# Products of field pairs by blocks in place of one row after another, and one PSUM tile of eight banks in place of eight buffers

## The chip, the cores and the metric

The kernel runs on one core of a Trainium2 chip. The metric is the device time of one execution in microseconds (us); the profile's span is about 1.9 us shorter. All runs told here were fast (no execution over 1.5% above the fastest of its kernel). A claim of "faster" or "slower" is made at 2%, with a 95% interval.

Names in the profile: PE is TensorE (matmuls), PEld its weight loads, DVE is VectorE, ACTq and SPq are the queues from which ScalarE and SyncE issue transfers. In the list of DMA queues, q1 carries the stores and the first two tiles' loads, q10 the other loads. The granted clock is TensorE's clock as a share of full speed. The ramp is the start of the program, until the first two tiles are under way; a fill is VectorE's work on one output buffer.

## The reference

```python
vid = jnp.einsum('bfd,de->bfe', x, W)          # x: (4096, 32, 64), W: (64, 64)
idx_i, idx_j = jnp.triu_indices(32, k=1)       # 496 pairs i < j
return x[:, idx_i, :] * vid[:, idx_j, :]       # (4096, 496, 64) float32
```

The output is 520 MB, the input 34 MB. There is one multiplication for each output element.

## The kernel before

The batch is cut into 16 tiles of 2 x 128 rows. In a tile, partitions are 2 halves x 64 embedding elements, and the free dimensions are fields (F = 32) and 128 batch rows (C). An output buffer (SLOT) holds 124 of the 496 pairs, so a tile fills four, and there are three of them. PSUM is the memory that matmuls write; four fields of `vid` fill one of its eight banks.

```python
    xpool = ctx.enter_context(tc.tile_pool(name="x", bufs=2))
    opool = ctx.enter_context(tc.tile_pool(name="out", bufs=3))
    psum = ctx.enter_context(
        tc.tile_pool(name="ps", bufs=8, space=bass.MemoryType.PSUM)
    )
    ...                                    # load(): x of a tile, in 4 pieces of 8 fields
    for t in range(NT):
        if 0 < t < NT - 1:
            loaded.append(load(t + 1, 4, nc.scalar))
        xt = loaded[t]
        vid = []
        for b in range(0, F, BANK):        # BANK = 4 fields, one PSUM bank
            pv = psum.tile([P, BANK, C], F32, tag="pv", name=f"pv_{t}_{b}")
            ...                            # two matmuls, one for each half of the partitions
            vid.append(pv)
        sent = 0
        for j in range(1, F):
            i = 0
            while i < j:
                ...                        # n pairs (i .. i+n-1, j), until the row or the buffer ends
                nc.vector.tensor_tensor(
                    ot[:, at - base : at - base + n, :],
                    xt[:, i : i + n, :],
                    vid[j // BANK][:, j % BANK : j % BANK + 1, :].to_broadcast([P, n, C]),
                    ALU.mult,
                )
                i += n
                at += n
                if t * NP + at == until or at in (base + SLOT, NP):
                    nc.sync.dma_start(     # the store: a whole buffer, in the first two tiles less
                        out=out[t][:, sent:at, :],
                        in_=ot[:, sent - base : at - base, :],
                    )
                    ...
```

## Time and profile before

| | before |
|---|---|
| time, median (lowest to highest) of 3 runs | 1298.64 us (1297.97 to 1299.37) |
| span of the profiled run | 1296.3 us |
| VectorE: instructions, busy | 544, 1098.1 us (85%) |
| VectorE: idle before its instructions | 158.3 us |
| TensorE: matmuls, busy | 512, 225.5 us |
| moved | 553.81 MB |

### The profile page before, as it was taken

What the parts mean: (1) busy time and instruction counts of PE and PEld (TensorE: products, weight loads), DVE (VectorE), ACT (ScalarE), POOL (GpSimd) and SP (SyncE); (2) the same over time, 40 slices, a digit from 0 to 9 for tenths busy, and PEclk for the clock granted to TensorE, in tenths of its full rate; (3) what the DMA queues carried; (4) which work ended last, traced back from release to release, by engine and by line L of the source; (5) the groups of instructions that cost most, each with busy time, mean ns of one, the idle gap of its engine ahead of it and who ended that gap; (6) DMA issues with size and microseconds to landing.
All of it is one profiled execution on the core that took longest, in us unless ns stands there. A gap on an engine that the chain in (4) does not pass through costs nothing.

```text
span 1296.3 us, 2062 instructions
## 1 busy us (share of the span) xinstructions
PE 225.5 (17%) x512; PEld 52.1 (4%) x512; DVE 1098.1 (85%) x544; POOL 0.2 (0%) x4
## 2 busy tenths in 40 slices
PE   4112131122121121211212112121121211212000
PEld 1000000000000000000000000000000000000000
DVE  7999999898798888988888888888888888979970
POOL 0000000000000000000000000000000000000000
PEclk8555555565555555655555565555555655555555
DMA  9999999999999999999999999999999999999996
GB/s 379 430 426 433 438 432 425 434 434 434 428 432 432 434 432 434 431 434 436 432 434 434 426 434 432 430 432 432 432 433 431 434 432 434 432 431 443 425 431 288
DMA packets 20891, 553.81 MB, mean 427 GB/s; under 512 B 2448, under 2 KB 2448, under 8 KB 10256
## 3 DMA queue, kind: packets, MB, share of 16 engines
q1 hardware_dynamic: 12816, 524.33, 93.8%
q10 hardware_dynamic: 8064, 29.36, 5.5%
q8 instruction: 4, 0.07, 0.0%
q14 instruction: 7, 0.06, 0.0%
HBM read 33.59 MB, written 520.09 MB: 427 GB/s over the span
## 4 chain that ended last, share of the span: by engine, by line
DMA 61%; DVE 34%; issue 1%; DVEq 0%; PE 0%; SPq 0%
DMA out_dram<-o 61%; DVE o L99 34%; DMA x<-in_r_x_dram 0%; DVEq L145 0%; PE pv L81 0%; DVEq L99 0%; SPq L56 0%
## 5 line engine op out<-in xcount | busy, mean ns | idle before, releaser
L99 DVE TENSOR_TENSOR o<-x,pv 128x2176 f32<-128x2176 f32 (+27 forms) x544 | 1098.1, 2093 | 158.3 <-DMA out_dram<-o 149.5
L81 PE MATMUL pv<-x,w 64*64 64x512 f32 x512 | 225.5, 1025 | 966.3 <-DMA x<-in_r_x_dram 887.2
L81 PEld LDWEIGHTS pv<-x,w 64*64 64x64 f32 x512 | 52.1, 208 | 1138.0 <-issue 1137.4
L128 POOL MEMSET const-bfloat16-1.0<- 128x1 bf16 x1 | 0.1, 102 | 0.0
L128 POOL MEMSET const-uint8-127<- 128x1 uint8 x1 | 0.1, 102 | 0.0
L128 POOL MEMSET const-float32-1.0<- 128x1 f32 x1 | 0.1, 99 | 0.0
L128 POOL MEMSET const-float32-0.0<- 128x1 f32 x1 | 0.1, 98 | 0.2 <-issue 0.2
## 6 DMA issues: line engine op xcount, KB each, us to landing
out_dram<-o SPq DMA_DIRECT2D x56, 7936.0 KB, 42.9
x<-in_r_x_dram ACTq DMA_DIRECT2D x56, 512.0 KB, 48.7
out_dram<-o SPq DMA_DIRECT2D x2, 3008.0 KB, 17.8
out_dram<-o SPq DMA_DIRECT2D x1, 5952.0 KB, 27.1
out_dram<-o SPq DMA_DIRECT2D x1, 4928.0 KB, 23.1
out_dram<-o SPq DMA_DIRECT2D x1, 4416.0 KB, 19.0
out_dram<-o SPq DMA_DIRECT2D x1, 4224.0 KB, 21.2
out_dram<-o SPq DMA_DIRECT2D x1, 3904.0 KB, 15.3
```

The lines of the kernel that those rows point to most:

```text
L81: nc.tensor.matmul(pv[half, :, :], lhsT=w2[half, :], rhs=xt[half, b : b + BANK, :], start=True, stop=True,)
L99: nc.vector.tensor_tensor(ot[:, at - base : at - base + n, :], xt[:, i : i + n, :], vid[j // BANK][:, j % BANK : j % BANK + 1, :].to_broad ...
L128: nc = _bacc.Bacc("TRN2", target_bir_lowering=False, num_devices=1, dynamic_dma_scratch_size=1024)
```

## The change

The intent is fewer VectorE instructions. In the old order each field j gives a row of j products, and buffer ends cut some, so 34 instructions a tile. In the new order pairs are grouped so that one instruction covers a block: within 16 fields, the pairs inside groups of 2, then across halves of groups of 4, of 8, of 16, and between the two 16s one block of 16 x 16. That is 22 instructions a tile. A block needs `vid` of fields in several banks at once, so `vid` becomes one tile over all eight banks. The first two tiles, whose stores start small and grow, keep the old order. The core of the diff:

```diff
+def by_block():
+    def within(lo):
+        yield "step", lo, 2, 1, 0
+        for k in range(2):
+            yield "step", lo, 4, 2, k
+        for k in range(4):
+            yield "step", lo, 8, 4, k
+        yield "row", lo + 8, lo, 8, 8
+    yield from within(0)
+    yield "row", 16, 0, 16, 16
+    yield from within(16)
 ...
-        tc.tile_pool(name="ps", bufs=8, space=bass.MemoryType.PSUM)
+        tc.tile_pool(name="ps", bufs=1, space=bass.MemoryType.PSUM)
     )
+    vid = psum.tile([P, F, C], F32)
 ...
-            pv = psum.tile([P, BANK, C], F32, tag="pv", name=f"pv_{t}_{b}")
 ...
-                    pv[half, :, :],
+                    vid[half, b : b + BANK, :],
 ...
-        for j in range(1, F):
-            ...
+        for at, m, w, i, di, j, dj in products(by_field() if t < 2 else by_block()):
+            ...
+            if m == 1:
+                left = xt[:, i : i + w, :]
+                right = vid[:, j : j + 1, :].to_broadcast([P, w, C])
+            else:
+                o = o.rearrange("p (m w) c -> p m w c", m=m)
+                right = vid[:, j : j + (m - 1) * dj + 1 : dj, :].unsqueeze(2).to_broadcast([P, m, w, C])
+                if di == 0:
+                    left = xt[:, i : i + w, :].unsqueeze(1).to_broadcast([P, m, w, C])
+                else:
+                    left = xt.rearrange("p (m d) c -> p m d c", d=di)[:, i // di : i // di + m, i % di : i % di + w, :]
+            nc.vector.tensor_tensor(o, left, right, ALU.mult)
```

`products` (cut here) cuts blocks where a buffer ends. The host undoes the new order of the pairs.

More of the change, by code (lines that the diff above doesn't have):

```diff
@@ L20, with by_field, products, pairs @@
 ]
-def first(j):
-    return j * (j - 1) // 2
+def by_field():
+    return [("row", j, 0, 1, j) for j in range(1, 32)]
+def by_block():
[9 more added lines that the diff above has]
+    yield from within(16)
+def products(blocks):
+    at = 0
+    for kind, a, b, c, d in blocks:
+        if kind == "row":
+            rows, n, i0, di, j0, dj = c, d, b, 0, a, 1
+        else:
+            rows, n, i0, di, j0, dj = 16 // b, c, a, b, a + c + d, b
+        r = k = 0
+        while r < rows:
+            room = SLOT - at % SLOT
+            if k or room < n:
+                m, w = 1, min(n - k, room)
+            else:
+                m, w = min(rows - r, room // n), n
+            yield at, m, w, i0 + r * di + k, di, j0 + r * dj, dj
+            at += m * w
+            if w == n or k + w == n:
+                r, k = r + m, 0
+            else:
+                k += w
+def pairs(blocks):
+    for at, m, w, i, di, j, dj in products(blocks):
+        for r in range(m):
+            for k in range(w):
+                yield i + r * di + k, j + r * dj
 @with_exitstack
@@ L73, in pairwise_bilinear_kernel @@
         xt = loaded[t]
-        vid = []
         for b in range(0, F, BANK):
-            pv = psum.tile([P, BANK, C], F32, tag="pv", name=f"pv_{t}_{b}")
             for h in range(2):
@@ L87, in pairwise_bilinear_kernel @@
                 )
-            vid.append(pv)
         sent = 0
-        for j in range(1, F):
-            i = 0
-            while i < j:
-                at = first(j) + i
-                base = at - at % SLOT
-                if at == base:
-                    ot = opool.tile([P, SLOT, C], F32, tag="o", name=f"o_{t}_{at}")
-                n = min(j - i, base + SLOT - at)
-                nc.vector.tensor_tensor(
-                    ot[:, at - base : at - base + n, :],
-                    xt[:, i : i + n, :],
-                    vid[j // BANK][:, j % BANK : j % BANK + 1, :].to_broadcast([P, n, C]),
-                    ALU.mult,
-                )
-                i += n
-                at += n
-                if t * NP + at == until or at in (base + SLOT, NP):
-                    nc.sync.dma_start(
-                        out=out[t][:, sent:at, :],
-                        in_=ot[:, sent - base : at - base, :],
-                    )
-                    sent = at
-                    if t * NP + at == until:
-                        until += next(growing, NT * NP)
+        for at, m, w, i, di, j, dj in products(by_field() if t < 2 else by_block()):
+            base = at - at % SLOT
+            if at == base:
+                ot = opool.tile([P, SLOT, C], F32, tag="o", name=f"o_{t}_{at}")
+            n = m * w
+            o = ot[:, at - base : at - base + n, :]
+            if m == 1:
+                left = xt[:, i : i + w, :]
+                right = vid[:, j : j + 1, :].to_broadcast([P, w, C])
+            else:
+                o = o.rearrange("p (m w) c -> p m w c", m=m)
+                right = vid[:, j : j + (m - 1) * dj + 1 : dj, :].unsqueeze(2).to_broadcast([P, m, w, C])
+                if di == 0:
+                    left = xt[:, i : i + w, :].unsqueeze(1).to_broadcast([P, m, w, C])
+                else:
+                    left = xt.rearrange("p (m d) c -> p m d c", d=di)[:, i // di : i // di + m, i % di : i % di + w, :]
+            nc.vector.tensor_tensor(o, left, right, ALU.mult)
+            at += n
+            if t * NP + at == until or at in (base + SLOT, NP):
+                nc.sync.dma_start(
+                    out=out[t][:, sent:at, :],
+                    in_=ot[:, sent - base : at - base, :],
+                )
+                sent = at
+                if t * NP + at == until:
+                    until += next(growing, NT * NP)
@@ L149 @@
     got = r.results[0]["out_0_dram"].reshape(NT, 2, D, _OUTS[0][0][1], C)
-    order = [first(j) + i for i in range(F) for j in range(i + 1, F)]
-    got = got.transpose(1, 0, 4, 3, 2)[:, :, :, order]
-    return _np.ascontiguousarray(got).reshape(_OUTS[0][0])
+    place = {p: k for k, p in enumerate((i, j) for i in range(F) for j in range(i + 1, F))}
+    res = _np.empty((2, NT, C, _OUTS[0][0][1], D), _np.float32)
+    for t in range(NT):
+        order = [place[p] for p in pairs(by_field() if t < 2 else by_block())]
+        res[:, t][:, :, order] = got[t].transpose(0, 3, 2, 1)
+    return res.reshape(_OUTS[0][0])
```

## The prediction

> **What bounds the kernel now.** I began with the page of the profile: the engines' busy time, the slices for the DMA engines, and the queues.
>
> ```profile
> PE 225.5 (17%) x512; PEld 52.1 (4%) x512; DVE 1098.1 (85%) x544; POOL 0.2 (0%) x4
> ...
> DMA  9999999999999999999999999999999999999996
> GB/s 379 430 426 433 438 432 425 434 434 434 428 432 432 434 432 434 431 434 436 432 434 434 426 434 432 430 432 432 432 433 431 434 432 434 432 431 443 425 431 288
> ...
> q1 hardware_dynamic: 12816, 524.33, 93.8%
> q10 hardware_dynamic: 8064, 29.36, 5.5%
> ```
>
> VectorE, which the change works on, is busy 85% of the span. The 16 DMA engines are busy at 90% or more in 39 of 40 slices, and the two data queues together take 93.8% + 5.5% = 99.3% of them. The rate is flat near 432 GB/s; only the first slice and the last differ much. So the DMA engines have about 0.7% of 1296.3 us, some 9 us, left, most of it at the two ends.
>
> The second view is the chain of waits in order of time, because its summary (DMA 61%, DVE 34%) could be read as if a third of the time were VectorE's to save.
>
> ```profile
> 698.38 17.67 DVE o L99 x16
> 716.06 42.61 DMA out_dram<-o
> 758.68 0.03 issue
> 758.73 0.04 issue
> 758.77 16.96 DVE o L99 x5
> 775.74 43.52 DMA out_dram<-o
> ...
> 819.36 17.02 DVE o L99 x6
> 836.40 44.37 DMA out_dram<-o
> ...
> 880.86 17.09 DVE o L99 x7
> ```
>
> The pattern is: VectorE fills one output buffer of 124 rows in about 17 us, the store of it lands some 43 us later, and its landing frees the buffer for a new fill. The chain visits every third buffer because there are three. A store of 7936 KB alone needs about 20 us of the DMA engines, so 43 us is two stores long: it queued behind an earlier one. The 17 us of VectorE in the chain lie beside other buffers' stores. If the fill ended sooner, the store would queue longer and land at the same time.
>
> Third, the waits between engines and the timeline of a steady tile:
>
> ```profile
> DVE o L99 <- DMA out_dram<-o: 149.5, 52, 5.0
> ```
>
> ```profile
> 536.80 17.66 DVE L99 TENSOR_TENSOR o<-x,pv 128x128 f32<-128x128 f32 x16 [3.16 <-DMA out_dram<-o]
> ...
> 541.74 3.68 PE L81 MATMUL pv<-x,w 64*64 64x512 f32 x8 [16.44 <-DMA x<-in_r_x_dram]
> ...
> 556.82 17.07 DVE L99 TENSOR_TENSOR o<-x,pv 128x1536 f32<-128x1536 f32 x7 [2.37 <-DMA out_dram<-o]
> ...
> 561.93 3.68 PE L81 MATMUL pv<-x,w 64*64 64x512 f32 x8 [16.51 <-DMA x<-in_r_x_dram]
> ...
> 582.03 3.68 PE L81 MATMUL pv<-x,w 64*64 64x512 f32 x8 [16.42 <-DMA x<-in_r_x_dram]
> ```
>
> At each buffer VectorE idles 2 to 3 us until an old store has landed; 149.5 of its 158.3 us of idle time are of this kind. The steady period of a tile follows from the chain: the fill of sixteen instructions starts at 698.38 and, three tiles later, at 940.82, so 242.44 / 3 = 80.8 us. VectorE needs 17.67 + 16.96 + 17.02 + 17.09 = 68.7 us of these. It could become 17% slower before it set the pace.
>
> **What the Trainium skill says.** "DMA: Bandwidth & Descriptors", section "Where 436 GB/s comes from", gives 435.2 GB/s as the ceiling of a core's 16 ports. The trace agrees: a window of three steady tiles moved 433 GB/s. The same section says that the HBM share of about 358 GB/s binds for transfers to and from HBM; this trace, of one core alone, does not show that. "VectorE: DVE Perf Modes", section "The TRN2 errata — SBUF-src ops pay a fixed extra latency per instruction", gives (N+151)/0.96 ns for an fp32 tensor_tensor, and its section "The perf-mode tier table (the rule you actually need)" one element a cycle for it whatever the memory. The groups by form agree:
>
> ```profile
> L99 DVE TENSOR_TENSOR o<-x,pv 128x3968 f32<-128x3968 f32 x16 | 68.5, 4281 | 0.0
> ...
> L99 DVE TENSOR_TENSOR o<-x,pv 128x128 f32<-128x128 f32 x16 | 4.6, 287 | 50.0 <-DMA out_dram<-o 41.7 <-PE pv L81 8.3
> ```
>
> The rule gives 4291 and 291 ns. "PSUM — Partial Sum Buffer", section "PSUM bank collisions raise a hardware error ⚠️", asks for synchronisation by bank, not by address. That decides what one tile of eight banks does; see below.
>
> **The change, part by part.** *Instructions.* From the third tile on there are 22 instead of 34 products a tile. The buffers of a tile get 9, 2, 2 and 9 of them instead of 16, 7, 6 and 5 in some order. All fills are 124 x 128 = 15872 elements, so the chain gives the exposed cost of one more instruction: (17.67 - 16.96) / (16 - 5) = 0.065 us, less than half of the fixed part in an instruction's own duration, because neighbours overlap. Twelve instructions fewer save 12 x 0.065 = 0.78 us a tile, 14 tiles 11 us. Busy VectorE goes from 1098 to about 1087 us, and the fills take about 17.2, 16.8, 16.8, 17.2 us. Those 11 us lie beside a store that ends later, so they come back as waiting: VectorE's idle time for stores goes from 149.5 to about 160 us. On the path to the end: 0.
>
> *Transfers.* Rows leave in another order, but in the same buffers of 124 rows and the same 7936 KB per store; loads keep their four pieces. 553.81 MB stays. The first two tiles, with their growing stores, keep their old order. So the ramp stays as well: 0.
>
> *PSUM.* One tile of eight banks takes the place of eight one-bank buffers. In the built list of instructions the matmuls of the changed kernel still wait bank by bank, or piece by piece, for VectorE, and products wait for matmuls in steps too. What moves is when a bank comes free. Banks 0 to 3 are free after row 120 of 496. Banks 4 and 5 are read until the last block of the tile, and banks 6 and 7 to its end. The loads' pieces arrive 20 us apart; counting 32 matmuls a tile, the group at 541.74 is the fourth piece of the tile whose products begin at 536.80. So the pieces come 55, 35 and 15 us before the start, and 5 us after it. The changed order needs the first two pieces at the start (35 us in hand less 4 us of matmuls), the third at row 120, 17 us in, and the fourth at row 248, two buffers or 40 us in. The third piece's matmuls now wait some 5 us for banks 4 and 5, still well ahead of their use. On the path: 0.
>
> Sum: 1298.6 us before, less 0, plus 0. I take 1298.5.
>
> **The rivals.** *The saving shows in full or in part.* For it: VectorE stands in the chain with 34%. If fills and stores were truly serial, about a third of the 11 us would show, 3 to 4 us, and 1295 us would come out. Against it: the DMA engines' 99.3%. The idle 0.7% caps any gain at 9 us; over 2% (26 us) is not to be had without fewer bytes or a higher rate.
>
> *VectorE becomes the bound,* because operands in four dimensions, with steps across PSUM banks and two broadcasts, run below one element a cycle. Below 17% it would be hidden. At 25% a tile would take about 86 us, 5 us over the period, and the time would be about 1298 + 14 x 5 = 1368 us. Against it: the innermost run is still 128 contiguous elements in all three operands, and today's broadcast of one row runs at full rate. The rate with bank-crossing steps no row of this trace shows.
>
> *The one PSUM tile serialises the tiles.* If every matmul waited for the last product of the tile before, 32 matmuls (four times 3.68 us) would stand between two tiles: 68 + 15 = 83 us against 80.8, so 13 x 2 = 26 us and some 1325 us. Against it: the waits by bank in the built kernel. Nor would a part of it show: the wait before each fill is 2 to 3 us, and one to two stores are queued at any time.
>
> *The load is late.* A step over banks 0 to 3 needs two whole pieces at once. It would take a delay of 30 us in the loads to show; their times sat steady to a microsecond from tile to tile, so I leave it 0.
>
> **Range and chances.** The three runs spread 1297.97 to 1299.37, and a different chip or day may give 0.3%, 4 us. A gain of 3 us is conceivable, and likewise some us if the loads interleave less well. That makes 1294 to 1302. Faster by over 2% is ruled out by the DMA engines' share short of an error of mine: 0.01. Slower by over 2% needs one of the two bad rivals: 0.02. Within 2%: 0.97.
>
> **What would show it.** Right: DMA still 99% over both queues and 432 GB/s in the slices; 376 products on VectorE (68 + 14 x 22) and busy time near 1087 us; its wait for stores near 160 us; 80.8 us from tile to tile in the chain; the 14336-element product close to (14336 + 151) / 0.96 = 15091 ns. Matmuls that wait for VectorE for about 5 us a tile and no product that waits for a matmul after the ramp would show the PSUM step right. Wrong: slices of DMA below 9 in the middle; products of 8192 or 14336 elements over 1.2 ns an element; or 15 us of matmuls in one run at a tile's start with VectorE idle beside them.

## The result, and the profile after

| | before | after |
|---|---|---|
| time, median (lowest to highest), runs | 1298.76 us (1297.97 to 1299.37), 4 | 1295.50 us (1295.05 to 1297.15), 4 |
| ratio after / before, 95% interval | | 0.9978 (0.9960 to 0.9995) |
| span of the profiled run | 1296.3 us | 1295.3 us |

Ratios here and below are the mean time of one kernel's fast runs over that of the other's fast runs of the same rounds, so not quite the ratio of the medians quoted.

The page of the changed kernel, engines, slices and queues:

```profile
PE 230.5 (18%) x512; PEld 49.1 (4%) x512; DVE 1087.2 (84%) x376; POOL 0.2 (0%) x4
...
DMA  9999999999999999999999999999999999999996
GB/s 376 432 427 434 437 434 425 435 434 432 433 431 434 432 435 432 432 430 436 430 432 433 433 429 432 434 436 431 431 433 433 434 432 434 435 429 423 437 439 290
...
q1 hardware_dynamic: 12816, 524.33, 93.9%
q10 hardware_dynamic: 8064, 29.36, 5.5%
```

VectorE has 168 instructions and 10.9 us of work less. The DMA row, the rates and the two queues are those of before: 93.9% + 5.5% = 99.4% of the engines' span.

The waits of the changed kernel: who waited for what, us in total, times, the longest one.

```profile
PE vid L128 <- DVE o L153: 128.8, 23, 24.1
DVE o L153 <- DMA out_dram<-o: 122.1, 40, 4.3
DVE o L153 <- issue: 37.4, 12, 3.5
DVE o L153 <- PE vid L128: 8.9, 2, 8.3
```

VectorE's wait for stores seems to fall, from 149.5 to 122.1 us. It did not: 37.4 us more are filed under "issue". These are 12 waits of about 3.1 us, and the timeline below shows one before the first fill of a tile, where before a store was named. In the kept trace each of the twelve ends 0.2 to 0.5 us after a store's last engine has landed. So they are waits for stores too, and together they are 159.5 us. A wait whose releaser the profile fails to find must be added back before two profiles are compared. With the 8.9 us of the ramp it is 168.4 us of idle time, 10.1 us more than before: all but 0.8 us of the 10.9 us saved.

The timeline of the changed kernel over the end of one steady tile and the start of the next:

```profile
515.54 17.20 DVE L153 TENSOR_TENSOR o<-x,vid 128x512 f32<-128x512 f32 x9 [3.35 <-DMA out_dram<-o]
...
520.66 1.97 PE L128 MATMUL vid<-x,w 64*64 64x512 f32 x4 [16.81 <-DMA x<-in_r_x_dram]
...
524.20 1.97 PE L128 MATMUL vid<-x,w 64*64 64x512 f32 x4 [1.56 <-DVE o L153]
535.92 17.20 DVE L153 TENSOR_TENSOR o<-x,vid 128x1024 f32<-128x1024 f32 x9 [3.18 <-issue]
```

Fills now take 17.20 us (nine products) and 16.75 us (two; 16.76 in the chain below). VectorE still waits about 3 us before each, 3.35 and 3.18 us before the two shown. The period stays too: one fill of two products starts at 475.16 and the same fill four tiles later at 798.09 (below), so 80.7 us a tile, for 80.8 before. The third piece's matmuls come in two groups: bank 4's start when the load lands at 520.66, bank 5's 1.56 us after those ended, when VectorE has read bank 5 for the last time.

The largest product by form in the changed kernel (busy us, mean ns, then idle time before it):

```profile
L153 DVE TENSOR_TENSOR o<-x,vid 128x14336 f32<-128x14336 f32 x28 | 422.2, 15083 | 44.7 <-DMA out_dram<-o 44.7
```

That is 1.052 ns an element, with an operand that spans two PSUM banks and two operands that repeat. Also the steps over several banks run at this rate: the 1024-element products took 1213 ns on average (in the tiles looked at, those over four banks as long as those over two, 1210 to 1220 ns), where the formula that the prediction quotes gives (1024 + 151) / 0.96 = 1224.

The chain of waits of the changed kernel, in order of time:

```profile
737.65 16.76 DVE o L153 x2
754.42 43.57 DMA out_dram<-o
798.09 16.76 DVE o L153 x2
814.87 25.25 DMA out_dram<-o
840.12 15.39 DVE o L153 x7
```

Here lies a trap. The page's summary of this chain gives DMA 55% and VectorE 39%, where before it gave 61% and 34%. VectorE works less and has the larger share. The reason is in the last two lines: once a tile the chain spends 25 us of the usual 43 with a store and then runs through seven products of a fill. Which releaser is inferred at such a point decides the shares; the DMA engines' work and the time are those of before. A share of the chain is not a saving that waits to be had.

### The profile page after: what moved, and what is told of

The parts are those of the page before. It is cut to its first block, busy times and chain, and to the rows that moved or that the text cites. A ratio compares the mean times of both kernels' runs of the same rounds, so it can differ in the third digit from the quotient of the medians.

```text
span 1295.3 us, 1845 instructions
## 1 busy us (share of the span) xinstructions
PE 230.5 (18%) x512; PEld 49.1 (4%) x512; DVE 1087.2 (84%) x376; POOL 0.2 (0%) x4
## 3 DMA queue, kind: packets, MB, share of 16 engines
q1 hardware_dynamic: 12816, 524.33, 93.9%
HBM read 33.59 MB, written 520.09 MB: 427 GB/s over the span
## 4 chain that ended last, share of the span: by engine, by line
DMA 55%; DVE 39%; issue 2%; PE 0%; DVEq 0%; SPq 0%
DMA out_dram<-o 55%; DVE o L153 39%; DMA x<-in_r_x_dram 0%; PE vid L128 0%; DVEq L193 0%; DVEq L153 0%; SPq L105 0%
## 5 line engine op out<-in xcount | busy, mean ns | idle before, releaser
L153 DVE TENSOR_TENSOR o<-x,vid 128x1024 f32<-128x1024 f32 (+15 forms) x376 | 1087.2, 2960 | 168.4 <-DMA out_dram<-o 122.1
L128 PE MATMUL vid<-x,w 64*64 64x512 f32 x512 | 230.5, 1035 | 960.2 <-DMA x<-in_r_x_dram 831.3
L128 PEld LDWEIGHTS vid<-x,w 64*64 64x64 f32 x512 | 49.1, 206 | 1139.9 <-issue 790.4
```

The lines of the kernel that those rows point to most:

```text
L128: nc.tensor.matmul(vid[half, b : b + BANK, :], lhsT=w2[half, :], rhs=xt[half, b : b + BANK, :], start=True, stop=True,)
L153: nc.vector.tensor_tensor(o, left, right, ALU.mult)
```

## The experiments

The theory: the 16 DMA engines set the pace; VectorE, TensorE and the loads each have slack, and what the change saves turns into waiting. The first rival: fills stand on the path, at least in part. Two more concern the PSUM tile and the loads. And the result itself asks whether 0.2% of gain is real, and which part gives it.

### VectorE slower on purpose: slow16 and slow32

On the changed kernel, 2048 elements (slow16) or 4096 (slow32) of each buffer's large product are computed twice; the result stays correct:

```diff
             nc.vector.tensor_tensor(o, left, right, ALU.mult)
+            if t >= 2 and n >= 64:
+                k = 16 // w            # slow32: 32 // w
+                nc.vector.tensor_tensor(o[:, :k], left[:, :k], right[:, :k], ALU.mult)
```

> The changed kernel with 2048 elements of each fill's large product computed twice: about 2.1 us + 0.07 us more VectorE work a fill, 56 fills, so busy 1087 + 122 = 1209 us and a fill of some 19.2 us against a period of 20.2. Theory (stores set the pace, VectorE has 3 us in hand a fill): hidden, 1295 to 1297 us. Rival (the fills stand on the path, as the 39% of VectorE in the chain suggests): a third to all of 122 us shows, 1336 to 1418 us.

Measured: 1296.86 us (1293.35 to 1300.54, 4 runs), ratio to the kernel before 0.9995 (0.9947 to 1.0043). VectorE busy is 1211.7 us, so 124.5 us were added. None of them shows in the ratio, whose interval leaves room for some 6 us either way (the four runs came in two pairs, near 1293.5 and near 1300.3 us). The engines of slow16, and its wait of VectorE for stores:

```profile
PE 228.2 (18%) x512; PEld 52.0 (4%) x512; DVE 1211.7 (93%) x432; POOL 0.2 (0%) x4
...
DVE o L153 <- DMA out_dram<-o: 39.7, 39, 1.7
```

It fell from 159.5 to 39.7 us: the added work came out of the waiting. That is the theory's number; the rival's least, 1336 us, is out.

> As slow16 with 4096 elements: 4.33 us more a fill, 21.3 us, over the period of 20.2. Theory: VectorE now sets the pace from the third tile on: start at 146, 14 tiles of 68.0 + 4 x 4.33 = 85.3 us, then one store of 20 us: 1360 us. The slices of DMA fall below 9 in the middle. Rival (fills on the path): 56 x 4.33 = 242 us in full, 1538 us.

Measured: 1360.45 us (1359.93 to 1360.51, 4 runs), ratio 1.0494 (1.0459 to 1.0529). The page of slow32, engines and DMA slices:

```profile
PE 214.3 (16%) x512; PEld 45.1 (3%) x512; DVE 1327.5 (98%) x432; POOL 0.2 (0%) x4
...
DMA  9999999998999989899898999999999999899898
```

VectorE is at 98%, its wait for stores is gone from the list of waits, and slices of DMA at 8 appear in the middle. The sum of fills gave 1360 us. So the slack that the prediction read from the profile, 17.2 of 20.2 us a fill, is the true one: at 19.2 us nothing happens, at 21.3 us the pace is VectorE's. The rival "VectorE becomes the bound" is a real mechanism; the change simply goes the other way.

### Fewer bytes: store120

On the changed kernel, from the third tile on 4 of each buffer's 124 rows are not stored; the result is wrong.

```diff
+                cut = 4 if t >= 2 else 0
                 nc.sync.dma_start(
-                    out=out[t][:, sent:at, :],
-                    in_=ot[:, sent - base : at - base, :],
+                    out=out[t][:, sent : at - cut, :],
+                    in_=ot[:, sent - base : at - base - cut, :],
                 )
```

> The changed kernel, but from the third tile on the last 4 of each buffer's 124 rows are computed and not stored (wrong result on purpose). 56 x 4 x 64 KB = 14.68 MB less at 432.8 GB/s is 33.9 us. Theory: 1261 to 1263 us, and VectorE's idle time falls by about the same 34 us to some 135. Rival (VectorE's fills on the path): less than half of it, over 1278 us.

Measured: 1264.71 us (1261.82 to 1266.58, 4 runs), ratio 0.9754 (0.9719 to 0.9790). The changed kernel did not run in the same call, so the ratios to the kernel before are compared: 0.9754 against 0.9966 to 0.9988 for the changed kernel (further below) is 27 to 30 us less, for 33.9 expected, with some 5 us of uncertainty. The profile is sharper: the two queues of store120 took 93.8% + 5.7% of 1260.0 us, which is 1254 us, where those of the changed kernel took 99.4% of 1295.3 us, 1288 us. That is 34 us less work for the DMA engines. VectorE's waits for stores in store120, the named part:

```profile
DVE o L153 <- DMA out_dram<-o: 96.9, 39, 3.1
```

With the 29.5 us under "issue" and 8.6 us of the ramp it idled 135.0 us, as expected. Less data made the kernel faster with VectorE's work unchanged. Less VectorE work, which is the change itself, did not, at 2%.

### The banks held: hold and serial

`hold` adds one tiny product at each tile's end that reads a column of all eight banks, so no matmul of the next tile may start earlier. `serial` adds the same at each tile's start too, so no product may start before all 32 matmuls.

```diff
+    touch = const.tile([P, 8, 1], F32)
 ...
+        if t >= 2:                     # at the tile's end; serial: also after the matmuls
+            nc.vector.tensor_tensor(touch, xt[:, 0:F:BANK, 0:1], vid[:, 0:F:BANK, 0:1], ALU.mult)
```

> The changed kernel with one tiny product at each tile's end that reads a column of all eight banks, so that no matmul of the next tile can start before (what a PSUM tile guarded as a whole would do to the matmuls). The first products of a tile then wait for banks 0 to 3: 16 matmuls, about 7.4 us. Theory: 68 + 8 = 76 us of 80.7 a tile, hidden, 1295 to 1297 us; the wait of products for matmuls rises from 9 us to some 100 us and their wait for stores falls by as much. Rival: each tile loses what the wait exceeds the 3 us of idle time at its start, 4.5 us x 13 = 58 us, 1354 us.

Measured: 1294.48 us (1292.90 to 1297.52, 4 runs), ratio 0.9969 (0.9953 to 0.9986). The waits of VectorE in hold:

```profile
DVE o L154 <- PE vid L129: 86.1, 15, 8.5
DVE o L154 <- DMA out_dram<-o: 82.3, 29, 3.7
```

They sum to 168.4 us, to the tenth what the changed kernel idled. The wait for matmuls took the place of waits for stores, and nothing else moved.

> As hold, with a second tiny product at each tile's start that reads all eight banks, so that no product runs before all 32 matmuls either: the rival of the prediction in full, put there at 1325 us. 68 + 15 = 83 us a tile over 80.7 gives that. But the fourth piece of the loads lands 5 us after the tile's start now, and the pieces come 20 us apart, so it may cost more: 4 to 5 us a tile more than 80.7, up to 1360 us.

Measured: 1296.43 us (1294.85 to 1297.02, 4 runs), ratio 0.9986 (0.9971 to 1.0001). This expectation was wrong: the full rival costs nothing. The waits of the tiny products and of the others in serial, and windows over one run of 32 matmuls between two tiles (window, its us, PE busy, PEld, DVE, POOL, granted clock, DMA share, GB/s; a DMA packet counts in the window in which it starts, so in short windows the share can exceed 1):

```profile
DVE touch L138 <- PE vid L129: 136.4, 14, 12.9
...
DVE o L156 <- DMA out_dram<-o: 24.1, 11, 2.9
```

```profile
613.40:617.40 4.00, 3.93 (x10) 1.21 (x12) 0.01 (x1) 0.00 (x0) 0.50 1.23 530
617.40:621.50 4.10, 4.10 (x16) 1.00 (x12) 0.00 (x0) 0.00 (x0) 0.82 1.00 430
621.70:623.70 2.00, 1.93 (x8) 0.47 (x8) 0.00 (x0) 0.00 (x0) 1.00 0.41 177
```

The 32 matmuls take 10.2 us, from 613.5 to 623.7, and not four times 3.68 us. The Trainium skill's page "TensorE: Matmul & The Clock Gate", section "What's actually happening", says that TensorE's clock is at half rate by default and released after about 3.4 us of sustained work. The trace agrees: a granted clock of 0.50 in the first 4 us, then 0.82 and 1.00, and the last eight matmuls took 1.93 us. The groups of eight that I had multiplied by four stand alone between loads; the two quoted in the prediction at 541.74 and 561.93 ran at 0.50. So 68.0 + 10.3 = 78.3 us a tile, under the period of 80.7, and it is hidden as all the rest.

### The load in one piece: load_whole

```diff
-            loaded.append(load(t + 1, 4, nc.scalar))
+            loaded.append(load(t + 1, 1, nc.scalar))
```

> The changed kernel with each x tile from the third on loaded in one transfer of 16 KB rows in place of four of 4 KB rows. In the trace a 4 KB packet of a load took 159 ns and a 15.9 KB packet of a store 592 ns, so 1792 packets of some 610 ns in place of 7168 of 159: 68.3 in place of 71.3 us on 16 engines, 3 us less. Theory (the DMA engines' busy time is the time): 1292 to 1293 us. If only bytes counted: 1295.5. If the load now holds up the tile's start: more than 1297.

Measured: 1308.13 us (1302.81 to 1309.58, 4 runs), ratio 1.0084 (1.0044 to 1.0123): some 11 us slower than the kernel before, where a gain was expected, 3 us over the changed kernel. The queues of load_whole:

```profile
q1 hardware_dynamic: 12816, 524.33, 93.7%
q10 hardware_dynamic: 2016, 29.36, 5.3%
```

The loads did get cheaper: 5.3% of 1306.6 us is 69 us, for 71 us before. But the stores' packets take 1224 us of the engines where they took 1216 us, and about 1% of the span is idle where 0.6 to 0.7% was. VectorE waits 170.6 us for stores, for up to 8.4 us at a time. So of the 11.3 us by which the span is longer than the changed kernel's, 6 us are longer work of the engines, and the rest is idle time of theirs: the last window below puts some 5 us of it at the end, where the 16 engines finish less evenly. Why a store's packets last longer when loads come in one piece is not settled by this run. The step that failed is my assumption that the engines' time is a sum of packet times that do not depend on each other, and that their idle time stays.

### Which part, if any, gives 0.2%: psum_only, order_8buf, and the same kernels again

`psum_only` is the kernel before with the one PSUM tile and nothing else. `order_8buf` has the new order with eight PSUM buffers, each block cut where a bank ends (the added `by_bank` does it), so 52 products a tile. `before_again`, `after_again`, `after_third` and `hold_again` are unchanged copies.

```diff
# psum_only, on the kernel before
-        tc.tile_pool(name="ps", bufs=8, space=bass.MemoryType.PSUM)
+        tc.tile_pool(name="ps", bufs=1, space=bass.MemoryType.PSUM)
+    vid = psum.tile([P, F, C], F32)
# order_8buf, on the changed kernel
-        for at, m, w, i, di, j, dj in products(by_field() if t < 2 else by_block()):
+        for at, m, w, i, di, j, dj in by_bank(by_field() if t < 2 else by_block()):
```

> The kernel before, unchanged, as a control. Ratio to itself 1.000 within 0.1%, some 1298.7 us. If two copies of one kernel differ by 0.2% on one chip, the 0.2% that the changed kernel gained is noise of the method.

> The changed kernel, unchanged, on a chip of this call. If the gain of 0.2% is real, 1295 to 1296.5 us and a ratio of 0.9975 to 0.999 with an interval below 1. If it was chance, a ratio that covers 1.

> Old order and 34 products a tile, with the one PSUM tile of eight banks. Theory (stores set the pace, nothing in the change lies on the path): 1298.5 us, ratio 0.999 to 1.001. If the small gain comes from the PSUM tile (fewer waits on TensorE), about 1295.5 us here.

> New order, eight PSUM buffers as before, so each block is cut where a bank ends: 52 products a tile in place of 34. VectorE busy some 14 x 18 x 0.065 = 16 us more than before, about 1114 us. If the small gain comes from fewer instructions, none here: 1298.5 to 1300 us. If it comes from the order of the rows (what is freed when), about 1295.5 us. If nothing is on the path, 1298.5.

> The changed kernel a third time, because the ratios so far, 0.9978 (0.9960 to 0.9995) and 0.9988 (0.9970 to 1.0006), leave open whether 0.1 to 0.2% of gain is real. If it is, 0.998 to 0.999 again with an interval below 1; if not, an interval that covers 1. Theory: no step on the path changed, so anything within 0.2% of 1 may come out.

> The kernel with the banks held to each tile's end, again: 0.9969 (0.9953 to 0.9986) before, the lowest ratio of all, though it only adds a wait. If chance between rounds, 0.998 to 1.001 here. If holding the matmuls back helps (TensorE busy 158 and not 230 us), 0.996 to 0.998 again and below the changed kernel of this call.

| run | products a tile | median us (lowest to highest), runs | ratio to the kernel before (95%) |
|---|---|---|---|
| before_again | 34 | 1297.86 (1296.33 to 1299.52), 5 | 1.0005 (0.9993 to 1.0018) |
| psum_only | 34 | 1296.16 (1293.61 to 1298.51), 5 | 1.0000 (0.9987 to 1.0014) |
| order_8buf | 52 | 1299.20 (1298.32 to 1300.07), 5 | 1.0015 (1.0003 to 1.0027) |
| after_again | 22 | 1297.45 (1291.78 to 1297.52), 6 | 0.9988 (0.9970 to 1.0006) |
| after_third | 22 | 1293.60 (1292.59 to 1295.38), 5 | 0.9966 (0.9951 to 0.9981) |
| hold_again | 23 | 1296.17 (1295.09 to 1297.17), 6 | 0.9986 (0.9972 to 1.0000) |

The first four ran on one chip, the last two on another. The control, before_again, came out at 1.0005: two copies of one kernel differ by less than the 0.2% in question. order_8buf's VectorE was busy for 1114.0 us, as expected. hold_again did not repeat the 0.9969 of hold, so holding the matmuls is not shown to help. The changed kernel's three ratios are 0.9978, 0.9988 and 0.9966. All lie below 1, and two intervals exclude it, so a gain of 0.1 to 0.3% is likely. The PSUM tile alone gives none of it, and more products go with a higher ratio. That speaks for the number of VectorE instructions, but slow16, with 124 us more of VectorE work, is at 0.9995 with an interval too wide to decide. And one kernel swings by as much: after_again had four runs of 1297.4 to 1297.5 us and two of 1291.8 and 1291.9.

The traces show where such differences sit. Below, the last 36 us of the span in the kernel before, the changed kernel, psum_only, slow16 and load_whole, in this order (same columns as above):

```profile
1260.30:1296.30 36.00, 0.00 (x0) 0.00 (x0) 0.00 (x0) 0.00 (x0) 0.50 0.67 291
```

```profile
1259.30:1295.30 36.00, 0.00 (x0) 0.00 (x0) 0.00 (x0) 0.00 (x0) 0.50 0.71 309
```

```profile
1255.80:1291.80 36.00, 0.00 (x0) 0.00 (x0) 0.00 (x0) 0.00 (x0) 0.50 0.80 346
```

```profile
1262.60:1298.60 36.00, 0.00 (x0) 0.00 (x0) 0.00 (x0) 0.00 (x0) 0.50 0.64 277
```

```profile
1270.60:1306.60 36.00, 0.00 (x0) 0.00 (x0) 0.00 (x0) 0.00 (x0) 0.50 0.57 247
```

In the last 36 us the engines fall idle one after the other. The idle part is 36 x (1 - share): 11.9, 10.4, 7.2 and 13.0 us in the first four, 15.5 us in load_whole. Subtract it from the four spans of 1296.3, 1295.3, 1291.8 and 1298.6 us, and 1284.4, 1284.9, 1284.6 and 1285.6 remain (1291.1 in load_whole). So a spread of 6.8 us in the span is one of 1.2 us without the tail. The view counts a packet where it starts, which makes the idle part 1 to 2 us too large, in all alike. The same stands in the queues: 99.3% of 1296.3 us and 94.1% + 5.6% of 1291.8 us are 1287 and 1288 us of work. What differs is how evenly the 16 engines finish. The last store's landings in the kept traces say it directly: in these four the first engine is done at 1283.2 to 1283.5 us, the last at 1291.0 to 1297.8.

The same subtraction places the small gain. Without the tail, the two traces of the kernel before have 1284.4 and 1285.4 us, and the three of the changed kernel 1284.9, 1285.5 and 1284.9. So in the traces no gain stands outside the tail, and the 0.1 to 0.3% of the ratios, if real, comes from how the engines finish. Why they finish more evenly in one execution than in another, and whether fewer products help that on average, stays open.

## Why the prediction was right

**The bound.** Shown. Taking away bytes saved time (store120), adding 124 us of VectorE work cost nothing that four runs can tell (slow16), and 4.3 us a fill cost what the sum of fills says (slow32: 1360 expected, 1360.45 measured).

**The instructions.** The step of 0.065 us for each instruction, from two fills with different counts, gave 1087 us of busy time and fills of 17.2 and 16.8 us; the trace has 1087.2, 17.20 and 16.75. The step itself rests on overlap, which the trace has: the products of the kernel before last 1138.8 us one by one, and VectorE was busy for 1098.1 us. The saving of 11 us came back as waiting: about 160 us expected for stores, 159.5 found once the unnamed waits are counted. The rate was expected at 15091 ns for the largest product and is 15083.

**The PSUM tile.** No product waits for a matmul after the ramp (8.9 us in two waits, 8.8 before), as predicted. The wait of the third piece's matmuls for VectorE was put at some 5 us a tile. In the profiled run the second half of them, those of bank 5, start 3.5 us after the load has landed (520.66 to 524.20), and TensorE idles for 1.6 us of these. In after_again, where the pieces come about 2 us earlier, both halves wait for VectorE (they start at 520.09 and 524.61). So the size was near, it hangs on when the load comes, and it has no effect.

**The rivals.** "The saving shows in part" gave 1295 us, and the first comparison came out at 1295.5. That nearness is no evidence for its mechanism. The tail holds the difference, and fills that grew by 124 us in all (slow16) left no trace in the time. A late load was not tested by itself; load_whole, which changes how loads arrive, still has no product waiting for a matmul after the ramp (9.1 us in two waits). The serial rival was mis-sized: I wrote 1325 us from four groups of 3.68 us, and it is 1296.4, because a long run of matmuls gets a higher clock. The rejection stood; its arithmetic did not.

**A loose reading.** The prediction gives a store of 7936 KB "alone" about 20 us. At 433 GB/s it is 18.8 us; 20.2 us is a store with its share of the loads. Nothing rests on the difference.

**The range.** 1294 to 1302 us held the result, but the point of 1298.5 is 3 us high, and a gain of 3 us was reckoned a matter of chips and chance, and it may be 0.1 to 0.3% of real gain.

## What to carry to other kernels

Before work is taken off an engine, ask what ends its idle time: where it waits for a buffer to be stored, what is saved turns into more waiting, and busy plus idle time stays. Measure slack by adding work on both sides of the expected knee; two runs settled here what shares of a chain could not. And compare whole waits: a part of them may be filed without a releaser in one of two profiles.

## What the Trainium skill lacked or had wrong

- "DMA: Bandwidth & Descriptors", section "Where 436 GB/s comes from": it says that for transfers between HBM and SBUF the HBM share of about 358 GB/s binds. One core alone moved 433 GB/s here over whole steady tiles, close to the page's ceiling of 435.2. The sentence lacks the condition that the page states for its table of measurements just before: about 358 GB/s is each core's share when both cores of a memory domain stream.
- The same page, section "Rules for kernel authors", asks for at least 1 MiB per DMA for most bandwidth. Four loads of 512 KB merged into one of 2 MB, beside a stream of large stores, made this kernel slower: ratio 1.0084 (1.0044 to 1.0123). The rule has no word on what merging loads does to stores that run beside them.
- No page seen gives a figure for how unevenly the 16 DMA engines end (the DMA page has only that two of them are usually slower). Here it was 7.2 to 15.5 us of mean idle time in the last 36 us of the span in the five traces shown, and in the first four nearly all of the spread of the spans.
- "VectorE: DVE Perf Modes", section "The TRN2 errata — SBUF-src ops pay a fixed extra latency per instruction": its formula holds beyond the sizes it names, at 14336 elements with a PSUM operand that spans two banks (15083 ns for 15091); at 512 elements, a size that the page names, the products here took 681 to 682 ns for the formula's 691. The page allows for a next instruction that starts earlier, but has no figure for it. Here a sum of durations overstates the cost of many instructions: one more cost 0.065 us, not 151 / 0.96 = 157 ns.
